# Which engine multiplies tokens by expert weights beside a recurrence, and the ranks of a planned schedule

## The chip, the cores and the metric

The kernel runs on one core of one Trainium2 chip, in one launch. The metric is device time in microseconds (us): the median of several executions. Besides, one execution is recorded by the hardware profiler, instruction by instruction; its own time and its span are given below. The engines are named as in the profile: PE is TensorE's matmul, PEld its weight load, DVE is VectorE, ACT is ScalarE, POOL is GpSimd, SP is SyncE.

## The reference

The input `x` is 8 sequences of 256 tokens of width 128, all in float32. Four stages follow each other, each added to its input after a layer normalisation:

```python
x = x + state_space(layernorm(x))      # a selective recurrence, 256 channels x 16 states
x = x + experts(layernorm(x))          # "p"
x = x + attention(layernorm(x))        # squared-relu attention with a gate, "a"
x = x + experts(layernorm(x))          # "r", with the same weights
```

The recurrence runs over the tokens of each sequence: `new = exp(A * d_t) * state + d_t * B_t * h_t`, and `y = sum_n new * C_t`. The expert layer has 8 experts of inner width 352; each token takes two of them, but all are computed and weighted:

```python
for e in range(8):
    w_e = sum(weights * (top_idx == e))            # 0 for experts not taken
    inter = (x @ w_up[e]) * silu(x @ w_gate[e])
    out = out + w_e[:, None] * (inter @ w_down[e])
```

## The kernel before, in words

The 8 sequences form four groups of two, so a group has 512 tokens. Activations are kept transposed: 128 features on the partitions, 512 tokens along the free dimension. For group g the work is cut into lanes (generators of operations):

- `s` (prelude, L516 on): normalisation, projection, convolution and step sizes of the recurrence. Its convolution on DVE, for groups 0 and 3, is L563.
- `m` (recurrence): 16 steps, each a multiplication (L744), a scan along tokens (L749) and a multiplication (L753) on DVE, all of 128 x 1024. The sum over states is made by DMAs that accumulate into a first buffer (lane `adder`, L716, issued on POOL's queue). Five buffers `st` exist; two hold the sums. ACT makes the decay factors (lane `feeder`, L697).
- `g`, `f`, `t`: the gate, the end of the recurrence (`y` on PE for groups 0 and 1, then a multiplication by the gate) and the projection back (`pb_m`).
- `r` (rest): expert layer p, attention a, expert layer r, with their normalisations and routers. Pieces of it are forked into lanes of their own. Group g's `r` starts after its `t` and after `r` of group g - 2.

So p0 means expert layer p of group 0. An expert layer folds the weight of an expert into the tokens: a row of weights, one per token, is broadcast to all partitions by a DMA (`fetched`, L969) into a buffer `wb` of 128 x 512, and `wb` is multiplied in place by the transposed tokens `xT` (`weighted`, L977). The up projection then reads `wb` in place of `xT`. The 8 x 352 inner columns are cut into 22 tiles of 128, so a tile can belong to two experts (then L993 instead of L986). For each tile PE makes the gate product (L487), ACT its silu (L960), PE the up product, DVE the product of both (`it`, L1000, one operand in PSUM), and PE the down product (L1006), two tiles later. The multiplication for an expert is issued when the expert two before it is through. Expert 0 of the layers named in `SOON` is not made in `weighted` but in the router's part, from PSUM (L940).

The order of all instructions is written by a planner (`Board`) at build time. It knows an estimated duration for each operation, keeps a time at which each engine becomes free, and each lane offers one operation. The one that can start first is taken; among those on the same engine that can start within the lane's `patience` of the first, the one with the lowest rank wins:

```python
first, lane = min(at, key=lambda x: x[0])
near = [
    l for t, l in at if l.op.engine == lane.op.engine and t <= first + l.patience
]
return min(near, key=lambda l: l.rank)
```

`RANKS` gives each kind of lane a rank per group (the group number breaks ties), and under "w" the patience of lanes `f` and of forked lanes. Where the planner sees PE idle for over 0.3 us ahead of a product, it fills the time with matmuls of the identity (L325). Each engine runs its instructions in the order written, and waits for semaphores where data come from elsewhere.

Of the kernel before, what the change touches and what calls it, by code (L numbers as in the profile page):

```python
# [10 lines left out]
ALU = mybir.AluOpType  # L11
# [84 lines left out]
def kernel(  # L96
# [27 lines left out]
    nc = tc.nc  # L124
# [23 lines left out]
    BEHIND = 2  # L148

    RANKS = {  # L150
        "s": [0, 4, 4, 1.5], "m": [1.5, 2, 3, 3.5],
        "g": [4, 0, 3.5, 2], "t": [0, 3.5, 3.5, 0.5],
        "r": [2, 0.5, 2.5, 0.5], "f": [2.5, 1.5, 4, 0.5], "w": [0, 0, 0.3, 0], "feeder": 5, "adder": 0,
    }
    SOON = ("p0", "p1", "r0", "p3", "r3")
    SPLIT = ()
    ENDS = 2
    assert E * F % P == 0 and all(cut >= P or cut % CG == 0 for _, cut in OWNER)
# [36 lines left out]
    for name, src in (  # L195
# [10 lines left out]
        n = src.shape[0]  # L206
# [75 lines left out]
    def ring(pool, shape, tag, name, bufs=1):  # L282

        held = rings.setdefault((pool.name, tag), [])
        free = held[-bufs].used if len(held) >= bufs else 0.0
        h = Held(pool.tile(shape, FP, tag=tag, name=name, bufs=bufs), free)
        held.append(h)
        return h
# [40 lines left out]
    def dve(us, out, ins, issue):  # L329
        return Op("DVE", us, out, ins, issue, lag=0.06)  # L330
# [4 lines left out]
    def pool(us, out, ins, issue):  # L335
        return Op("POOL", us, out, ins, issue, lag=0.06)

    def load(us, out, ins, issue, queue="SP", take=0.1):
        return Op(queue, take, out, ins, issue, lag=us)

    def mm(n):
        return 0.005 + 0.00167 * n
# [4 lines left out]
    def dve_us(n):  # L347
        return 0.08 + 0.0012 * n
# [22 lines left out]
    for k in range(K):  # L371
# [6 lines left out]
    PARTS = [  # L378
        [(b, b + 1) for b in range(n)] if g in SPLIT else [(0, n)] for g, n in enumerate(SIZES)
    ]  # L380
# [137 lines left out]
    def prelude(g):  # L518
# [64 lines left out]
        shut(ps)  # L583
        bc = Held(dram.tile([2 * N, G], FP, tag="bc", name=f"bc_{g}"))
        yield load(2.4, [bc], [ww], lambda: nc.sync.dma_start(bc.ap, xpj[R:XW, :]))


# [78 lines left out]
    def feeder():  # L666

        for g in range(NG):
# [6 lines left out]
            for q in range(N // NC):  # L675
# [4 lines left out]
                for tag, r0 in (("bt", q * NC), ("ct", N + q * NC)):  # L680
                    t = ring(scan, [P, NC, G], tag, f"{tag}_{g}_{q}", bufs=2)
                    yield load(4.0, [t], [bc], lambda: nc.sync.dma_start(
                        t.ap, bc.ap[r0 : r0 + NC, :].partition_broadcast(P)
                    ))
                    rows_at.append(t)
# [23 lines left out]
    def adder():  # L709

        while len(done & {f"f{g}" for g in range(NG)}) < NG:
            if not sums:
                yield None
                continue
            g, us, acc, st, into, of = sums.pop(0)
            yield load(us, [acc], [st], lambda: nc.gpsimd.dma_start(  # L716
                into, of, accum_op=ALU.add
            ), "POOL", 0.9)
            st.used = max(st.used, acc.ready)
            landed[g] = landed.get(g, 0) + 1  # L720
            if st is not acc:
                st.open = False
# [98 lines left out]
    def parted(g, tile):  # L821
        return tile, [Held(tile.ap[:, tokens(g, p)], tile.used) for p in range(len(PARTS[g]))]

    def whole(tile, parts):

        tile.ready = max(h.ready for h in parts)
        tile.used = max(h.used for h in parts)
        return tile
# [15 lines left out]
    def led_in(g, which, key, p, shared):  # L844
# [31 lines left out]
        if "we" not in shared:  # L876
# [8 lines left out]
            ]  # L885
            if f"{which}{g}" in SOON:
                shared["wb"] = parted(g, ring(
# [38 lines left out]

        if f"{which}{g}" not in SOON:
            return
# [16 lines left out]
    def moe(g, which, key, shared, ends):  # L945

        nm = f"{which}{g}"
        NT = SIZES[g] * TT
        G = NT * P
        xT, we = (whole(*shared[k]) for k in ("xT", "we"))  # L950
# [5 lines left out]
        def gate(i):  # L956
            gp = bank([P, G], f"gp_{nm}_{i}")
            yield pe(mm(G), [gp], [xT], product(gp.ap, [(wg_sb[:, i * P : (i + 1) * P], xT.ap)]))
            sg = ring(ffn, [P, G], f"sg{key}", f"sg_{nm}_{i}", bufs=SG)
            yield act(act_us(G), [sg], [gp], lambda: nc.scalar.activation(  # L960
                sg.ap, gp.ap, AF.Silu, bias=zero
            ), SILU)
            shut(gp)
            sgs[i] = sg
# [9 lines left out]
        def weighted(e):  # L974

            wb = wx[e]
            yield dve(dve_us(G), [wb], [xT], lambda: nc.vector.tensor_mul(wb.ap, wb.ap, xT.ap))  # L977

        def up(i, cols_of, sg, wa, wn, it, width):
# [49 lines left out]
        for i in range(LEAD):  # L1029
            yield from gate(i)  # L1030
        ahead = which + str(g) in SOON
        if not ahead:
# [3 lines left out]
        if not ahead:  # L1036
            yield from weighted(0)
        yield from weighted(1)

        dns = [  # L1040
# [4 lines left out]
        for i in range(NK - ENDS):  # L1045
            if i + LEAD < NK:
                yield from gate(i + LEAD)
            e, cut = OWNER[i]
            its[i] = tile_of(i)
            yield from up(i, everything, sgs.pop(i), wx[e], wx.get(e + 1), its[i], G)  # L1050
            if cut <= P:

                if e + WB < E:
                    yield from fetched(e + WB)
                if e + 2 < E:
                    yield from weighted(e + 2)
            if i >= BEHIND:
                it = its.pop(i - BEHIND)
                for p, dn in enumerate(dns):
                    yield from down(i - BEHIND, dn, it, tokens(g, p))  # L1060
# [250 lines left out]
```

## Time and profile before

| | us |
|---|---|
| median of 3 runs (759.11 to 759.85) | 759.33 |
| the profiled execution | 758.34 |
| its span, first to last instruction | 756.6 |
| PE busy, of which L325 | 737.7, 133.2 |
| DVE busy | 568.6 |
| ACT busy | 431.1 |
| POOL busy | 89.8 |

The clock granted to PE was 0.999 over the span. Busy times are unions over the span and say nothing of what waits for what; the filler L325 counts as busy PE. In the trace the 64 scans of the recurrences start between 41 and 511 us: those of group 0 from 41 to 118, of group 1 from 123 to 221, of group 2 from 235 to 373, of group 3 from 379 on. The first expert product of p0 is at 158 us, and the layers end as follows (L479, the addition of a layer's output): p0 at 232 us, p1 at 352, r0 at 419, r1 at 492, p2 at 542, p3 at 634, r2 at 704, r3 at 752.

### The profile page before, as it was taken

To read this page: it belongs to the slowest core of one execution; us is meant where nothing else is said; L and a number is where in the kernel's file an instruction comes from. 1 tells how busy PE (TensorE), PEld (TensorE's weight loads), DVE (VectorE), ACT (ScalarE), POOL (GpSimd) and SP (SyncE) were. 2 spreads that over 40 slices of the span, in tenths; PEclk is the share of its full clock that TensorE was granted. 3 is DMA by queue.
4 is the path that set the end of the run, shared out by engine and by line. 5 is a ranking of instruction groups with operands and counts; after the bars stand their busy time and mean duration, and the time that the engine had idled before them with its cause. 6 is when DMAs were issued, how large, how long until landed. Compare 5 with 4: busy or idle time off the path is not lost.

```text
span 756.6 us, 8464 instructions
## 1 busy us (share of the span) xinstructions
PE 737.7 (98%) x3093; PEld 403.6 (53%) x3093; DVE 568.6 (75%) x824; ACT 431.1 (57%) x570; POOL 89.8 (12%) x110
## 2 busy tenths in 40 slices
PE   4999999999999999999999999999999999999997
PEld 3877996853446744434754533443555434644343
DVE  2599999999999999899999998995735334354332
ACT  5578333799947879977876677742252322432220
POOL 2021110311112210002120110011100001000000
PEclk9999999999999999999999999999999999999999
DMA  8719795399763345655774666745011200000110
GB/s 260 209 57 220 169 219 162 98 228 218 166 171 84 76 124 133 166 133 138 176 170 96 159 161 179 160 102 109 2 42 27 72 15 14 15 29 29 47 36 14
DMA packets 38903, 88.63 MB, mean 117 GB/s; under 512 B 4339, under 2 KB 14542, under 8 KB 38862
## 3 DMA queue, kind: packets, MB, share of 16 engines
q0 software_dynamic: 9312, 30.94, 22.8%
q1 hardware_dynamic: 20624, 41.54, 17.2%
q10 hardware_dynamic: 8926, 15.61, 6.8%
q8 instruction: 24, 0.39, 0.2%
q14 instruction: 17, 0.14, 0.0%
HBM read 55.71 MB, written 1.44 MB: 76 GB/s over the span
## 4 chain that ended last, share of the span: by engine, by line
PE 78%; DVE 15%; ACT 3%; issue 2%; ACTq 0%; DVEq 0%
PE gp_r L487 10%; PE dn_r L1006 10%; PE dn_p L1006 9%; PE gp_p L487 9%; PE up_r L986 7%; PE up_p L986 7%; DVE st L749 6%; PE up_r L993 3%; DVE st L744 3%; PE up_p L993 3%; DVE st L753 2%; PE av_a L1197 2%; PE tp_p L325 1%; PE xpj L325 1%; PE v_a L1131 1%
## 5 line engine op out<-in xcount | busy, mean ns | idle before, releaser
L749 DVE TENSOR_TENSOR_SCAN st<-decay,st 128x1024 f32<-128x1024 f32 x64 | 147.8, 2309 | 2.5
L960 ACT ACTIVATE sg_r<-gp_r,zero 128x512 f32<-128x512 f32 x88 | 59.9, 687 | 109.8 <-PE gp_r L487 88.7
L57 ACT ACT_TABLE_LOAD x89 | 114.2, 1283 | 8.0 <-PE dn_r L1006 3.6
L697 ACT ACTIVATE decay<-dl,zero,a_sb 128x510 f32<-128x510 f32 x128 | 96.2, 804 | 36.9 <-DVE st L749 35.7
L1000 DVE TENSOR_TENSOR it_r<-up_r,sg_r 128x512 f32<-128x512 f32 x88 | 60.4, 687 | 66.7 <-PE up_r L986 42.3
L960 ACT ACTIVATE sg_p<-gp_p,zero 128x512 f32<-128x512 f32 x88 | 59.3, 685 | 62.5 <-PE gp_p L487 46.6
L1000 DVE TENSOR_TENSOR it_p<-up_p,sg_p 128x512 f32<-128x512 f32 x88 | 60.3, 686 | 43.4 <-PE up_p L986 29.4
L1006 PE MATMUL dn_p<-it_p,wd_sb 128*128 128x512 f32 x176 | 91.2, 605 | 0.6 <-DVE it_p L1000 0.6
L1006 PE MATMUL dn_r<-it_r,wd_sb 128*128 128x512 f32 x176 | 90.5, 603 | 0.0
L716 POOL DMA_DIRECT2D st<-st x58 | 50.4, 874 | 334.2 <-DVE st L753 303.7
L487 PE MATMUL gp_r<-xT_r,wg_sb 128*128 128x512 f32 x176 | 90.0, 597 | 0.0
L487 PE MATMUL gp_p<-xT_p,wg_sb 128*128 128x512 f32 x176 | 89.0, 594 | 0.0
L744 DVE TENSOR_TENSOR st<-bt,du 128x1024 f32<-128x1024 f32 x64 | 78.8, 1231 | 0.0
L753 DVE TENSOR_TENSOR st<-st,ct 128x1024 f32<-128x1024 f32 x64 | 78.1, 1221 | 0.7
L986 PE MATMUL up_p<-wb_p,wu_sb 128*128 128x512 f32 x128 | 65.1, 594 | 0.0
L986 PE MATMUL up_r<-wb_r,wu_sb 128*128 128x512 f32 x128 | 64.9, 592 | 0.0
L1006 PEld LDWEIGHTS dn_p<-it_p,wd_sb 128*128 128x128 f32 x176 | 31.3, 189 | 47.1 <-issue 36.3
L487 PEld LDWEIGHTS gp_r<-xT_r,wg_sb 128*128 128x128 f32 x176 | 32.6, 190 | 42.7 <-issue 37.4
L1006 PEld LDWEIGHTS dn_r<-it_r,wd_sb 128*128 128x128 f32 x176 | 31.6, 190 | 44.3 <-issue 39.5
L487 PEld LDWEIGHTS gp_p<-xT_p,wg_sb 128*128 128x128 f32 x176 | 32.8, 190 | 41.2 <-issue 36.3
L325 PEld LDWEIGHTS y<-ident 128*128 128x128 f32 x428 | 48.0, 192 | 1.2 <-PE dt L487 0.8
L325 PE MATMUL y<-ident 128*128 128x128 f32 x428 | 48.2, 275 | 0.0
(217 smaller groups left out, 853.1 us busy)
## 6 DMA issues: line engine op xcount, KB each, us to landing
st<-st POOLq DMA_DIRECT2D x54, 512.0 KB, 6.4
bt<-bc SPq DMA_DIRECT2D x32, 512.0 KB, 6.0
ct<-bc SPq DMA_DIRECT2D x32, 512.0 KB, 4.5
wb_r<-wrow_r ACTq DMA_DIRECT2D x30, 256.0 KB, 3.8
wb_p<-wrow_p ACTq DMA_DIRECT2D x29, 256.0 KB, 3.9
st<-h POOLq DMA_DIRECT2D x6, 256.0 KB, 4.9
wg_sb<-in_L_ffn_w_gate_dram SPq DMA_DIRECT2D x2, 704.0 KB, 4.7
wu_sb<-in_L_ffn_w_up_dram SPq DMA_DIRECT2D x2, 704.0 KB
```

The source lines that it names most:

```text
L57: self.load_tables(op.table)
L325: nc.tensor.matmul(ps[:, 0:n], lhsT=ident[:, 0:m], rhs=ident[:, 0:n], start=True, stop=True)
L487: nc.tensor.matmul(ps, lhsT=lhsT, rhs=rhs, start=(i == 0), stop=(i == len(terms) - 1))
L697: nc.scalar.activation(shaped[:, n, :, 1:], delta[c].ap.rearrange("p (b t) -> p b t", b=GB)[:, :, 1:], AF.Exp, bias=zero, scale=a_sb[:, c, ...
L716: yield load(us, [acc], [st], lambda: nc.gpsimd.dma_start(into, of, accum_op=ALU.add), "POOL", 0.9)
L744: yield dve(1.22, [st], [bt, du[c]], lambda: nc.vector.tensor_mul(st.ap, bt.ap, du[c].ap.unsqueeze(1).to_broadcast([P, NC, G])))
L749: yield dve(2.29, [st], [das[c]], lambda: nc.vector.tensor_tensor_scan(flat, das[c].ap.rearrange("p n t -> p (n t)"), flat, 0.0, ALU.mult, ...
L753: yield dve(1.22, [st], [ct], lambda: nc.vector.tensor_mul(st.ap, st.ap, ct.ap))
L960: yield act(act_us(G), [sg], [gp], lambda: nc.scalar.activation(sg.ap, gp.ap, AF.Silu, bias=zero), SILU)
L986: nc.tensor.matmul(ps.ap, lhsT=wu_sb[:, i * P : (i + 1) * P], rhs=wa.ap[:, cols_of], start=True, stop=True,)
L1000: yield dve(dve_us(width), [it], [ps, sg], lambda: nc.vector.tensor_mul(it.ap, ps.ap, sg.ap[:, cols_of]))
L1006: yield pe(mm(dn.ap.shape[1]), [dn], [it], lambda: nc.tensor.matmul(dn.ap, lhsT=wd_sb[:, i, :], rhs=it.ap[:, cols_of], start=(i == 0), sto ...
```

## The change

In the five expert layers p0, r0, p1, r1 and p2, the multiplication of `wb` by `xT` is issued on GpSimd (`nc.gpsimd.tensor_tensor`) instead of VectorE, and the planner is told a duration of 0.1 + 0.0024 x 512 = 1.33 us for it (0.69 us for the one on DVE). In p3, r2 and r3 it stays on DVE. The ranks change: of `s` for groups 1 and 3, `m` 2, `g` 2, `t` 2, `r` 0 and 1, `f` 1 and 2, the patience of group 1 (0 to 0.6) and the rank of the adder. A key "late" is added. The arithmetic is the same.

```diff
     RANKS = {
-        "s": [0, 4, 4, 1.5], "m": [1.5, 2, 3, 3.5],
-        "g": [4, 0, 3.5, 2], "t": [0, 3.5, 3.5, 0.5],
-        "r": [2, 0.5, 2.5, 0.5], "f": [2.5, 1.5, 4, 0.5], "w": [0, 0, 0.3, 0], "feeder": 5, "adder": 0,
+        "s": [0, 1.5, 4, 3], "m": [1.5, 2, 3.5, 3.5],
+        "g": [4, 0, 1.5, 2], "t": [0, 3.5, 4, 0.5],
+        "r": [1, 0, 2.5, 0.5], "f": [2.5, 3, 3, 0.5], "w": [0, 0.6, 0.3, 0], "late": 2, "feeder": 5, "adder": 1.5,
     }
     SOON = ("p0", "p1", "r0", "p3", "r3")
+
+    SPARED = ("p0", "r0", "p1", "r1", "p2")
...
+    def pool_us(n):
+        return 0.1 + 0.0024 * n
...
         def weighted(e):
 
             wb = wx[e]
+            if nm in SPARED:
+                yield pool(pool_us(G), [wb], [xT], lambda: nc.gpsimd.tensor_tensor(
+                    wb.ap, wb.ap, xT.ap, ALU.mult
+                ))
+                return
             yield dve(dve_us(G), [wb], [xT], lambda: nc.vector.tensor_mul(wb.ap, wb.ap, xT.ap))
```

## The prediction

> **What bounds the kernel now.** I read the page's busy times first, then the table of stages, then the chain, then single instructions on GpSimd (POOL) and VectorE (DVE).
>
> ```profile
> PE 737.7 (98%) x3093; PEld 403.6 (53%) x3093; DVE 568.6 (75%) x824; ACT 431.1 (57%) x570; POOL 89.8 (12%) x110
> PE 78%; DVE 15%; ACT 3%; issue 2%; ACTq 0%; DVEq 0%
> ```
>
> The first line has busy us, share and count of each engine; the second shares out the chain that ended last. TensorE (PE) seems full, but line 325 is the filler: multiplications of the identity that the planner puts wherever it sees PE idle. So the stages must be read with that line beside them. The first table has the busy time of every engine in five stretches, the second the filler alone.
>
> ```profile
> 40.00:128.00 88.00, 86.86 (x631) 73.77 (x630) 86.02 (x61) 47.02 (x64) 14.40 (x15) 1.00 0.69 169
> 128.00:160.00 32.00, 31.42 (x189) 23.27 (x189) 31.31 (x53) 22.29 (x31) 8.11 (x8) 1.00 0.57 131
> 160.00:280.00 120.00, 119.08 (x488) 64.02 (x487) 115.48 (x170) 96.41 (x124) 22.05 (x21) 1.00 0.62 153
> 280.00:520.00 240.00, 239.74 (x812) 110.25 (x813) 219.06 (x277) 173.64 (x213) 31.34 (x35) 1.00 0.62 147
> 520.00:756.00 236.00, 231.47 (x791) 108.66 (x789) 100.06 (x221) 68.94 (x106) 8.48 (x8) 1.00 0.11 30
> ```
> ```profile
> 160.00:280.00 120.00, 18.11 (x146) 17.71 (x144) 1.00 0.62 153
> 280.00:520.00 240.00, 10.96 (x90) 10.75 (x90) 1.00 0.62 147
> 520.00:756.00 236.00, 4.38 (x32) 4.20 (x32) 1.00 0.11 30
> ```
>
> After stretch and length the columns are PE, weight loads, DVE, ACT, POOL. From 40 to 160 us DVE is full (117.3 of 120) with the first recurrence and the start of the second, and there is no expert layer yet. From 160 to 280, beside recurrences, DVE is busy 115.5 of 120 and PE spends 18.1 us on filler: DVE sets the pace. From 280 to 520 DVE has 20.9 us idle and PE only 11.0 us of filler; both are near their limit. After 520 the recurrences are over and PE alone decides. So DVE time is worth its full price from 160 to 280, part of it to 520, nothing later, and no more than 18.1 + 11.0 = 29.1 us of filler can be won beside recurrences.
>
> **Part 1: the multiplication leaves DVE.** Line 977 has 59 instances. The layers named are p0, r0, p1 (seven each, expert 0 being made earlier, on DVE, at line 940) and r1, p2 (eight each): 37. They are the first 37 in the trace, 8 between 160 and 280 us and 29 to 526. One takes 682 ns (median), but back to back the next DVE instruction starts 0.60 us after it, so DVE is relieved of 37 x 0.60 = 22.2 us.
>
> **What comes back.** GpSimd has run no such multiplication, but it runs an addition of the same shape with two operands in SBUF, line 494: 1.27 us at least, 3.32 at most. Five of its eight lie beside a recurrence. Here are three of them (two GpSimd and DVE pairs, then a DVE multiplication of line 977 itself):
>
> ```profile
> 143.77 1.26 POOL L494 TENSOR_TENSOR x<-x,b_first 128x512 f32<-128x512 f32 x1 [0.71 <-ACT xn_m L437]
> 144.13 1.99 DVE L744 TENSOR_TENSOR st<-bt,du 128x1024 f32<-128x1024 f32 x1
> 253.38 1.26 POOL L494 TENSOR_TENSOR x<-x,b_first 128x512 f32<-128x512 f32 x1 [2.35 <-ACT xn_m L437]
> 253.53 1.41 DVE L899 TENSOR_TENSOR pair_p<-pr_p 128x256 f32<-128x256 f32 x1
> 358.03 1.39 POOL L494 TENSOR_TENSOR x<-x,b_back 128x512 f32<-128x512 f32 x1
> 358.45 1.53 DVE L977 TENSOR_TENSOR wb_r<-wb_r,xT_r 128x512 f32<-128x512 f32 x1
> ```
>
> Columns are start, duration, engine, line. Line 744 usually takes 1.22 us and took 1.99; line 899 takes 0.42 and took 1.41; line 977 takes 0.68 and took 1.53. The two others stretched a scan (2.29 us) to 3.18 and 2.76. Each of the five lengthened one DVE instruction, by 0.77, 0.99, 0.85, 0.89 and 0.47 us: mean 0.79. Lines 744 and 749 have no other long instance. The DVE operations hit read two operands in SBUF; at 639.57 us the same addition ran beside a line 1000 product, which reads one operand in PSUM, and that kept its 0.69 us. Most DVE time beside the moved work is of the first kind: lines 744, 749 and 753 alone fill 68 of the 115 busy us between 160 and 280.
>
> So a moved multiplication frees 0.60 us of DVE and takes about 0.79 back: +0.19 each, +7.0 us of DVE in all. The bounds are 0 taken back (it always falls beside line 1000), a gain of 22.2, and 1.27 taken back, a loss of 37 x 0.67 = 24.8; I take 0.79, since all five seen in this company paid. On the path: the eight before 280 us count fully, 8 x 0.19 = +1.5. The 29 later ones make 5.5, and 20.9 us of idle DVE time can cover them; I let a quarter through, +1.4 (5.5 without that cover).
>
> The Trainium skill, page "SBUF — State Buffer", section "SBUF: two separate sides", says that the shared ports are an exclusive lock held for the whole instruction, and that the other engine fully blocks. By that wording a loss could reach the whole 1.27 us each time; the rows show 0.47 to 0.99, because DVE often starts its instruction after GpSimd did, so the measured mean stands in the sum.
>
> **Latency of the product.** DVE gave it 0.68 us after the row's landing, GpSimd gives it 1.3 to 3.3. It is issued an expert ahead: 2.75 tiles of three products at 0.86 us (two matmuls 0.43 apart), 7.1 us of PE work. That hides it; uncovered, each would cost up to 2.6 us. I cost it at nothing. In r1 and p2 expert 0 goes this way too, with less lead, but another layer's matmuls are there to run.
>
> **GpSimd's queue.** It is in order. It gains 37 x 1.3 = 48 us and was 12% busy. Behind a multiplication waits the next accumulate (line 716, 0.86 us to issue, 6.4 to land), hence a buffer `st`. Three of the five rotate; a step comes every 360/42 = 8.6 us between 160 and 520 (42 scans of line 749), so a buffer has 25.7 us, of which 4.7 are work and 7.3 the accumulate. 13 us of slack hide up to 3.3 us of delay. Uncovered it would stall DVE by that delay. The other way round the multiplication stands behind accumulates that wait for DVE; this is the second rival.
>
> **Part 2: the ranks.** They reorder DVE, ACT and PE where several lanes are ready at the same instant; `late` is read nowhere. Three moves touch something the trace shows late.
> - `r` of group 0 goes from 2 to 1, below `s` of group 3 (1.5 to 3). At 262 to 269 us the six line 563 operations of prelude 3 (4.5 us) run on DVE ahead of r0's layernorm, while PE fills 26 times (3.06 us) ahead of `tp_r`. With r0 first that filler can go: 0 to -3.1, I take -1.5.
> - `f` of group 1 goes from 1.5 to 3, behind r0. Its `y` products (1.95 us of PE, twice) and with them tail 1 and layer p1 wait for PE's work in r0: 0 to +3.9, I take +1.0, since p0 is nearly over then.
> - Patience 0.6 for group 1's forks: PE may be left idle up to 0.6 us for about 29 of their steps, counted in the code: 0 to +17. Most find their operand there already; I take +1.0.
> - The rest (`s` 1 and 2, `m` 2, `g` 2, `t` 2, `f` 2, the adder) changes ties between lanes that are rarely ready together, or work for which the next stage waits on something else: 0 in the sum. An order that shifts everywhere can still move several us either way, and this is the largest unknown: -8 to +10, judged by the 9.1 us of PE filler between 360 and 440 us, where r0, a1 and r1 run short of products, and its mirror image.
>
> **Sum.** 758.34 (profiled execution: span 756.6 and 1.7 around it) + 1.5 + 1.4 - 1.5 + 1.0 + 1.0 = 761.7. The median of the runs, 759.33, is 1.0 above the profiled execution: **762.7 us**.
>
> **Rivals.**
> - *Faster.* The relief holds: GpSimd mostly runs beside line 1000, or the new order uses what DVE gets. For it: 18.1 us of filler between 160 and 280 with DVE full. Against it: five of five stretched. If a third of the 29.1 us of filler becomes products: 759.3 - 9.7 = 749.6. It decides from the point at which DVE loses under 0.5 us per multiplication, or at which the ranks alone win over 5 us. Chance 0.42.
> - *GpSimd's order.* Its accumulates wait for DVE 37 times between 160 and 520 us, 248.7 us in all and 12.5 at the longest. DVE will lag the written order by 29 us of blocking that the planner doesn't count, so a multiplication can stand behind an accumulate until its 7.1 us of cover is gone, and PE, in order too, stops: up to 12.5 - 7.1 = 5.4 us. Three such stops: 762.7 + 16 = 779. Chance 0.10.
> - *No change.* Blocking and relief cancel and the order wins as much as it loses: 759. Chance 0.09. That the edit does nothing is excluded: the layers' names match and the ranks are read.
>
> **How the numbers follow.** The forecast has 0.39, so slower by over 0.2% (1.5 us, about what a measurement of this kernel can tell from no change) has 0.39 + 0.10 = 0.49, within it 0.09, faster 0.42. The range reaches from the faster rival less half its gain again, 745, to just below the queue's stops, 776; the forecast's own range is 761 to 771.
>
> **What would show it.** Right: line 977's 37 instances on POOL at 1.3 us or more; lines 744, 749 and 753 with instances 0.5 to 1.2 us too long, 25 to 35 us in sum, about 10 of them before 280 us; DVE busy about 7 us more than 568.6; PE's filler between 160 and 520 near 29 us. Wrong: line 744 at 1.22 throughout, DVE busy down by 20 us, or filler there under 20 us. If POOL's accumulates wait as now but PE waits on `wb`, the queue is the cause.

## The result, and the profile after

The changed kernel takes 763.68 us (median of 4, 762.95 to 765.5) against 759.49 before in the same comparison: ratio 1.0059, 95% interval 1.004 to 1.0078. The prediction was 762.7. The profiled execution took 763.30 with a span of 761.5. The helper functions moved the lines: the filler is now L327, the steps of a recurrence L749 (multiplication), L754 (scan) and L758 (multiplication), the product `it` L1010, the down product L1016, the accumulate L721, and the moved multiplication is L983 on GpSimd (L987 where it stayed on VectorE).

First the page of the changed kernel: busy us, share and count of each engine, and the engines' shares of the chain that ended last ("issue" is time in which the engine waited for nothing that the profile shows).

```profile
PE 735.5 (97%) x3037; PEld 395.9 (52%) x3037; DVE 576.1 (76%) x787; ACT 431.7 (57%) x570; POOL 144.1 (19%) x147
PE 62%; DVE 22%; issue 9%; ACT 2%; POOL 2%; DMA 1%; DVEq 0%; ACTq 0%; POOLq 0%
```

Thirty-seven instructions have left DVE, and it is busy 7.5 us longer (568.6 before). Its share of the chain went from 15% to 22%, PE's from 78% to 62%, and "issue" from 2% to 9%. Next the stages (after start, end and length: PE, weight loads, DVE, ACT, POOL), and then the filler alone.

```profile
160.00:280.00 120.00, 114.68 (x466) 61.82 (x465) 115.64 (x144) 96.11 (x120) 35.91 (x30) 1.00 0.62 154
280.00:520.00 240.00, 236.17 (x782) 105.08 (x782) 226.31 (x265) 173.12 (x214) 70.04 (x64) 1.00 0.62 148
520.00:761.50 241.50, 237.44 (x792) 108.58 (x790) 101.55 (x222) 71.75 (x110) 10.14 (x9) 1.00 0.09 29
```
```profile
160.00:280.00 120.00, 18.29 (x149) 18.34 (x150) 1.00 0.62 154
280.00:520.00 240.00, 7.32 (x59) 6.92 (x58) 1.00 0.62 148
520.00:761.50 241.50, 0.83 (x6) 0.83 (x6) 1.00 0.09 29
```

From 160 to 280 us DVE is as full as before with 26 fewer instructions, and PE now stands still for 5.3 us (0.9 before), on top of as much filler. Between 280 and 520 the filler is 3.6 us less, but PE stands still for 3.8 us (0.3 before). Filler is idle time that the planner saw coming; standing still is what it did not expect. The groups of instructions by line and form (count, then busy us and mean ns) say where DVE's time went:

```profile
L754 DVE TENSOR_TENSOR_SCAN st<-decay,st 128x1024 f32<-128x1024 f32 x64 | 156.0, 2437 | 3.3 <-DVE st L749 0.5
L749 DVE TENSOR_TENSOR st<-bt,du 128x1024 f32<-128x1024 f32 x64 | 90.8, 1419 | 0.0
L983 POOL TENSOR_TENSOR wb_p<-wb_p,xT_p 128x512 f32<-128x512 f32 x22 | 35.6, 1635 | 7.6 <-DMA wb_p<-wrow_p 7.6
L983 POOL TENSOR_TENSOR wb_r<-wb_r,xT_r 128x512 f32<-128x512 f32 x15 | 22.6, 1509 | 12.6 <-DMA wb_r<-wrow_r 12.6
```

The same 64 scans took 147.8 us before, the same 64 multiplications 78.8. Single instructions of the changed kernel show how (start, duration, engine, line):

```profile
178.53 1.56 POOL L983 TENSOR_TENSOR wb_p<-wb_p,xT_p 128x512 f32<-128x512 f32 x1
178.15 3.04 DVE L749 TENSOR_TENSOR st<-bt,du 128x1024 f32<-128x1024 f32 x1
197.14 2.78 POOL L983 TENSOR_TENSOR wb_p<-wb_p,xT_p 128x512 f32<-128x512 f32 x2
196.76 3.73 DVE L637 TENSOR_TENSOR dl<-dl,ww 128x512 f32<-128x512 f32 x1
```

A multiplication of 1.22 us took 3.04 beside one of GpSimd's, and one of 0.69 took 3.73 beside two in a row. Below, *stretch* is the sum over DVE instructions of what each took above the median of its line and shape, where that is over 0.1 us. It was 4.0 us before (all beside GpSimd's additions) and is 34.2 now: 30.2 more, 0.82 for each of the 37. Not all of the instructions hit read two tensors: six are the normalisation L427, with one tensor and scalars per partition as input, at 0.65 to 1.39 us instead of 0.34, 4.0 us in sum. None is a product `it` (L1010, one operand in PSUM): 19 of these ran beside a multiplication on GpSimd for over 0.2 us, and the longest took 0.69.

PE feels it through the product `it`. The first line is the wait of the weight load ahead of a down product in the kernel before, the second in the changed one (total us, times, longest):

```profile
PEld dn_p L1006 <- DVE it_p L1000: 8.4, 14, 1.4
```
```profile
PEld dn_p L1016 <- DVE it_p L1010: 16.4, 20, 2.3
```

### The profile page after: what moved, and what is told of

Read it like the earlier page. It is cut to its first block, busy times and chain, and to the rows that moved or that the text cites. A ratio compares the mean times of both kernels' runs of the same rounds, so it can differ in the third digit from the quotient of the medians.

```text
span 761.5 us, 8378 instructions
## 1 busy us (share of the span) xinstructions
PE 735.5 (97%) x3037; PEld 395.9 (52%) x3037; DVE 576.1 (76%) x787; ACT 431.7 (57%) x570; POOL 144.1 (19%) x147
## 3 DMA queue, kind: packets, MB, share of 16 engines
q0 software_dynamic: 9312, 30.94, 22.6%
## 4 chain that ended last, share of the span: by engine, by line
PE 62%; DVE 22%; issue 9%; ACT 2%; POOL 2%; DMA 1%; DVEq 0%; ACTq 0%; POOLq 0%
PE dn_p L1016 8%; PE gp_r L492 8%; DVE st L754 8%; PE dn_r L1016 8%; PE gp_p L492 8%; PE up_p L996 6%; PE up_r L996 6%; DVE st L749 5%; DVE st L758 4%; PE up_p L1003 3%; PE up_r L1003 2%; PE av_a L1207 1%; DVE it_r L1010 1%; PE xpj L327 1%; DMA st<-st 1%
## 5 line engine op out<-in xcount | busy, mean ns | idle before, releaser
L754 DVE TENSOR_TENSOR_SCAN st<-decay,st 128x1024 f32<-128x1024 f32 x64 | 156.0, 2437 | 3.3 <-DVE st L749 0.5
L1010 DVE TENSOR_TENSOR it_r<-up_r,sg_r 128x512 f32<-128x512 f32 x88 | 59.6, 684 | 67.8 <-PE up_r L996 49.8
L721 POOL DMA_DIRECT2D st<-st x58 | 50.9, 882 | 272.6 <-DVE st L758 205.5
L1010 DVE TENSOR_TENSOR it_p<-up_p,sg_p 128x512 f32<-128x512 f32 x88 | 59.7, 683 | 49.3 <-PE up_p L996 27.1
L1016 PE MATMUL dn_p<-it_p,wd_sb 128*128 128x512 f32 x176 | 91.0, 606 | 4.0 <-DVE it_p L1010 4.0
L1016 PE MATMUL dn_r<-it_r,wd_sb 128*128 128x512 f32 x176 | 90.3, 601 | 1.2 <-DVE it_r L1010 1.2
L749 DVE TENSOR_TENSOR st<-bt,du 128x1024 f32<-128x1024 f32 x64 | 90.8, 1419 | 0.0
L758 DVE TENSOR_TENSOR st<-st,ct 128x1024 f32<-128x1024 f32 x64 | 80.5, 1258 | 0.9
L1016 PEld LDWEIGHTS dn_p<-it_p,wd_sb 128*128 128x128 f32 x176 | 31.2, 189 | 51.1 <-issue 30.7
L1016 PEld LDWEIGHTS dn_r<-it_r,wd_sb 128*128 128x128 f32 x176 | 31.7, 190 | 42.4 <-issue 35.1
L327 PEld LDWEIGHTS y<-ident 128*128 128x128 f32 x470 | 52.8, 192 | 1.2 <-PE dt L492 0.8
L327 PE MATMUL y<-ident 128*128 128x128 f32 x470 | 53.1, 275 | 0.0
```

The source lines that it names most:

```text
L327: nc.tensor.matmul(ps[:, 0:n], lhsT=ident[:, 0:m], rhs=ident[:, 0:n], start=True, stop=True)
L721: yield load(us, [acc], [st], lambda: nc.gpsimd.dma_start(into, of, accum_op=ALU.add), "POOL", 0.9)
L749: yield dve(1.22, [st], [bt, du[c]], lambda: nc.vector.tensor_mul(st.ap, bt.ap, du[c].ap.unsqueeze(1).to_broadcast([P, NC, G])))
L754: yield dve(2.29, [st], [das[c]], lambda: nc.vector.tensor_tensor_scan(flat, das[c].ap.rearrange("p n t -> p (n t)"), flat, 0.0, ALU.mult, ...
L758: yield dve(1.22, [st], [ct], lambda: nc.vector.tensor_mul(st.ap, st.ap, ct.ap))
L1010: yield dve(dve_us(width), [it], [ps, sg], lambda: nc.vector.tensor_mul(it.ap, ps.ap, sg.ap[:, cols_of]))
```

## The experiments

The theory: GpSimd's multiplications hold up DVE for as long as they relieve it or longer, DVE paces PE here, and the ranks matter little. The main rival: blocking is absorbed and the ranks make the loss. A second one: GpSimd's queue in order makes `wb` late. Ratios are to the kernel before in the same comparison, whose median lay between 759.1 and 759.7 us; all kernels but the two named memset compute the same.

| kernel | us | ratio to before (95%) | DVE busy | stretch |
|---|---|---|---|---|
| before | 759.5 | 1 | 568.6 | 4.0 |
| changed | 763.68 | 1.0059 (1.004 to 1.0078) | 576.1 | 34.2 |
| engine_only | 786.3 | 1.0351 (1.0336 to 1.0365) | 575.0 | 32.3 |
| ranks_only | 765.74 | 1.0081 (1.0068 to 1.0094) | 569.8 | 3.9 |
| memset | 750.76 | 0.9888 (0.9873 to 0.9903) | 548.1 | 3.7 |
| memset2 | 750.92 | 0.9889 (0.9876 to 0.9903) | 548.3 | 4.2 |
| same_order_dve | 754.84 | 0.9935 (0.9923 to 0.9948) | 568.0 | 3.9 |
| gp_p0 | 759.56 | 0.9997 (0.9989 to 1.0006) | 573.2 | 13.4 |
| gp_rest | 757.65 | 0.9978 (0.9969 to 0.9988) | 570.5 | 24.5 |
| old_ranks_dve | 778.13 | 1.0243 (1.023 to 1.0257) | 568.4 | 4.2 |
| undo_w1 | 784.31 | 1.0329 (1.0314 to 1.0345) | 580.6 | 38.5 |
| undo_r0_s3 | 778.54 | 1.0256 (1.024 to 1.0271) | 584.3 | 42.1 |
| blocking_told | 774.74 | 1.0203 (1.0186 to 1.022) | 585.9 | 42.4 |
| searched_dve | 750.03 | 0.9875 (0.9858 to 0.9891) | 567.8 | 4.8 |

### Each half of the change alone

```diff
# engine_only: the changed kernel with the ranks of before
# ranks_only: the changed kernel with no layer spared
-    SPARED = ("p0", "r0", "p1", "r1", "p2")
+    SPARED = ()
```

> The old ranks, and the 37 multiplications on GpSimd. If the shared ports give back what VectorE is relieved of (the prediction's theory): VectorE instructions stretched by 25 to 35 us in sum, VectorE busy 574 to 577 us, and 760 to 764 us, 0 to 4 us slower than before. If the ranks alone made the kernel slower and the blocking is absorbed (rival one): 755 to 759 us, at or below before.

> The new ranks, and all multiplications on VectorE. Prediction's theory: the ranks are worth about +0.5 us in sum, so 758 to 762 us, and no VectorE instruction longer than usual beyond the 4 us in sum of before. Rival one (the ranks are the whole loss): 763 to 766 us.

Neither theory had this. The multiplications on GpSimd with the old ranks cost 27 us, the new ranks without them 6.6, and both together 4.2. The stretch with the old ranks is 32.3 us and DVE busy 575.0, as expected; the time is 22 us above the expected 760 to 764. So the halves don't add up: the planner writes the order from the ranks and from the price and engine that it is told, and that order had to be parted from the engine that does the work.

### The order without the engine

```diff
# same_order_dve (the changed kernel's plan); old_ranks_dve (the same with the ranks of before)
-                yield pool(pool_us(G), [wb], [xT], lambda: nc.gpsimd.tensor_tensor(
+                yield pool(pool_us(G), [wb], [xT], lambda: nc.vector.tensor_tensor(
```

The planner still believes in GpSimd and 1.33 us; the instruction goes to VectorE at that place.

> The changed kernel's order as the planner wrote it with GpSimd's 1.33 us, but the 37 multiplications issued on VectorE at that place. Prediction's theory: VectorE gets 22 us of work back and loses 30 us of blocking, so 758 to 763 us, a little faster than the changed kernel, although its order was planned for another engine. If the relief of VectorE is real and blocking harmless: slower than the changed kernel, 767 us or more.

> The old ranks, the planner told that the 37 multiplications run on GpSimd for 1.33 us, but all issued on VectorE. It parts the 786.3 us of old ranks with GpSimd: if the order is what is bad, 774 to 781 us (786.3 less the 9 us that the engine costs in the other order); if blocking weighs more in that order, 757 to 768.

The changed kernel's order with all work on VectorE takes 754.84 us, 4.3 us less than before (759.09 in that comparison) and 8.8 us less than the changed kernel (9.4 by the two ratios, as the runs of before differ a little). That is below the expected 758 to 763: the theory had the direction, not the size. The order with old ranks and the new price takes 778.13: there the order is what is bad, as the first reading had it, and GpSimd adds 786.3 - 778.1 = 8.2 us. So in both orders the engine costs 8 to 9.4 us, and with VectorE doing all of it the four orders stand so:

| | planned on VectorE | planned on GpSimd |
|---|---|---|
| old ranks | 759.5 | 778.1 |
| new ranks | 765.7 | 754.8 |

The old ranks are good with the engine and price of VectorE, the new ones with GpSimd's, and each set loses 11 to 19 us with the other. PE's filler shows it; first old_ranks_dve, then same_order_dve:

```profile
160.00:280.00 120.00, 26.37 (x218) 26.05 (x218) 1.00 0.67 162
280.00:520.00 240.00, 15.45 (x130) 15.27 (x130) 1.00 0.60 142
520.00:640.00 120.00, 5.65 (x50) 5.38 (x50) 1.00 0.08 23
```
```profile
160.00:280.00 120.00, 19.50 (x158) 19.35 (x158) 1.00 0.64 155
280.00:520.00 240.00, 6.11 (x48) 5.91 (x48) 1.00 0.62 148
520.00:640.00 120.00, 0.00 (x0) 0.00 (x0) 1.00 0.10 29
```

The sums are 47.5 and 25.6 us: 21.9 of the 22.9 us between the spans (776.2 and 753.3) are idle time that the planner itself had written in.

### Is it the reading, the occupancy or the lateness?

```diff
# memset; memset2 writes 0.2 and then 0.1. What is left out is the product itself.
-                yield pool(pool_us(G), [wb], [xT], lambda: nc.gpsimd.tensor_tensor(
-                    wb.ap, wb.ap, xT.ap, ALU.mult
-                ))
+                yield pool(pool_us(G), [wb], [xT], lambda: nc.gpsimd.memset(wb.ap, 0.1))
```

> The changed kernel in its own order, but GpSimd writes a constant into wb in place of multiplying it, so it reads no SBUF there (the experts' outputs are then those of a constant input). Prediction's theory: with no second reader the stretching of VectorE falls from 34 us to under 8, VectorE busy from 576 to about 548 us, and the time by 4 to 10 us, to 754 to 760. Rival one: stretching is absorbed elsewhere, and the time stays at 762 to 765. Rival two (GpSimd's queue in order is what delays): the write is shorter than the product, about 0.5 us by the other writes of this kernel, so the time falls by 2 us or less with PE still waiting on wb.

> The changed kernel's order; GpSimd writes two constants into wb, one after the other, in place of the product (the experts' input is a constant). GpSimd is then held about as long as by a product (two writes of 0.5 to 0.9 us against 1.57), but reads nothing. If the shared read path is the cost: VectorE stretched by under 8 us, 750 to 754 us, within 3 us of the single write. If GpSimd's occupancy or the lateness of wb were the cost: 757 to 763 us.

Groups of the single write (memset), then of the double one (memset2):

```profile
L754 DVE TENSOR_TENSOR_SCAN st<-decay,st 128x1024 f32<-128x1024 f32 x64 | 147.2, 2301 | 3.3 <-DVE st L749 0.5
L749 DVE TENSOR_TENSOR st<-bt,du 128x1024 f32<-128x1024 f32 x64 | 78.6, 1228 | 0.0
L983 POOL MEMSET wb_p<- 128x512 f32 x22 | 15.5, 707 | 19.0 <-DMA wb_p<-wrow_p 19.0
```
```profile
L749 DVE TENSOR_TENSOR st<-bt,du 128x1024 f32<-128x1024 f32 x64 | 78.7, 1230 | 0.0
L983 POOL MEMSET wb_p<- 128x512 f32 x44 | 27.0, 615 | 17.0 <-DMA wb_p<-wrow_p 14.5 <-PE dn_p L1014 1.3
L983 POOL MEMSET wb_r<- 128x512 f32 x30 | 19.0, 634 | 14.2 <-DMA wb_r<-wrow_r 12.6 <-PE tp_r L457 0.7
```

In an unchanged order the stretch is gone and the time falls by 13 us, more than the 4 to 10 expected. Two writes in place of one, 46 us on GpSimd against 58 for the products, change nothing (750.92 against 750.76). So GpSimd's occupancy is not the cost. Nor is the lateness of `wb`: PE's waits for it sum to 2.2 us in the changed kernel and to 2.3 in the same order on VectorE, and the second rival falls. What costs is an operation on GpSimd that reads SBUF beside DVE; the writes leave out the reading and the arithmetic together, and no run parts these two. The Trainium skill, page "SBUF — State Buffer", section "Who interferes with whom", states that a DVE instruction with two SBUF inputs contends with a GpSimd instruction that reads SBUF and not with one that only writes it; the 34.2 us of stretch against 3.7 and 4.2 agree.

### Early and late multiplications

```diff
# gp_p0: the seven of p0 on GpSimd, 30 on VectorE. gp_rest: the other way round ("!=")
-                yield pool(pool_us(G), [wb], [xT], lambda: nc.gpsimd.tensor_tensor(
+                yield pool(pool_us(G), [wb], [xT], lambda: (nc.gpsimd if nm == "p0" else nc.vector).tensor_tensor(
```

> The changed kernel's order, the seven multiplications of p0 on GpSimd, the other 30 on VectorE. The prediction let the early ones, from 160 to 280 us, count in full: at 30 us of stretching for 37 (0.82 each, less 0.60 of relief) that is +1.5 us over the 754.8 of all on VectorE, 755.5 to 758. If stretched instructions do not matter for the path here: 754 to 755.

> The same order, with p0's seven on VectorE and the other 30 on GpSimd. If, as the prediction had it, idle VectorE time covers three quarters of the later ones: +1.4 us over 754.8, 755 to 757. If nearly all of VectorE's net loss reaches the end also beyond 280 us: +5 to +8 us, 760 to 763.

The order is that of same_order_dve, so 754.84 is the base. The seven of p0 cost 4.7 us, the thirty others 2.8 (3.3 if the ratios are compared); together 7.5 of the 8.8. Both miss: the early ones cost more than expected, the late ones less than the rival reading and more than the prediction's. The stretch tells why. For the seven it is 13.4 - 3.9 = 9.5 us, 1.35 each, which less 0.60 of relief is 5.3 us; for the thirty 24.5 - 3.9 = 20.6, 0.69 each, which is 2.6 us. DVE busy rises by 5.2 and 2.5. So for p0 DVE's net loss reaches the end nearly one to one, and the early multiplications lose more of it. For the thirty others the medians say the same, less surely: the twelve executions spread from 755.82 to 759.78, the profiled one is the lowest of them, and the intervals of the two ratios leave 1.6 to 4.9 us.

PE's wait for a late `it` moves with the engine. The weight loads ahead of down products waited in the layers p as follows, first in same_order_dve, then in gp_p0:

```profile
PEld dn_p L1016 <- DVE it_p L1010: 5.4, 10, 0.8
```
```profile
PEld dn_p L1016 <- DVE it_p L1010: 16.1, 19, 2.3
```

With p0's seven on GpSimd the wait in the layers p is nearly that of the changed kernel (16.4), and the one in the layers r is 1.3 us, as in same_order_dve. With the thirty others there it is the other way round: 5.9 in the layers p, 6.3 in the layers r (6.2 in the changed kernel).

### The ranks one by one, and a planner that is told

```diff
# undo_w1 (the rest of RANKS, here and below, is left out: ...)
-        ... "w": [0, 0.6, 0.3, 0] ...
+        ... "w": [0, 0, 0.3, 0] ...
# undo_r0_s3
-        "s": [0, 1.5, 4, 3], ... "r": [1, 0, 2.5, 0.5] ...
+        "s": [0, 1.5, 4, 1.5], ... "r": [2, 0, 2.5, 0.5] ...
# blocking_told
+                yield dve(0.82, [], [], lambda: None)
                 yield pool(pool_us(G), [wb], [xT], lambda: nc.gpsimd.tensor_tensor(
```

> The changed kernel with the patience of group 1's forked lanes back at 0. The prediction charged the patience with +1.0 us, so without it 762 to 763 us. Rival: the patience is a large part of what makes the new order good (the written order gains 4.3 us over before when VectorE does the work): 768 us or more without it.

> The changed kernel with the ranks of group 0's expert lanes and of prelude 3 as before (2 and 1.5), so prelude 3 goes first again. The prediction credited the move with 1.5 us: 764 to 766 us without it. Rival: ranks are worth whatever the whole order comes to, not the local filler: outside 760 to 768.

> The changed kernel, its planner told of 0.82 us of VectorE time for each of GpSimd's multiplications (the measured mean of the stretching), in front of each. If the loss comes from blocking that the planner does not know: a planner that knows it writes an order that loses less, under 761 us. If the planner's price merely shuffles the order: anywhere from 760 to 780 us, with the same 30 us of stretching.

Taking back the patience costs 20.6 us over the changed kernel, taking back r0 and prelude 3 costs 14.9: in both the rival reading holds, by far. Both orders also have more stretch (38.5 and 42.1 us against 34.2) and more filler (137.8 and 133.5 us over the span against 126.1), so these figures mix what the order costs PE with what it makes GpSimd cost DVE. With `f` of group 1 alone put back to 1.5 the planner writes the same program. The planner that was told of the blocking wrote a worse order (774.74) with more stretch (42.4). That the ranks were not chosen for that price is one reading; whether ranks chosen for it would do better was not tried.

### A faster version

```diff
# searched_dve: same_order_dve with other ranks (the lines that these replace are left out)
+    RANKS = {'s': [0, 1.5, 4, 3], 'm': [2.0, 1.0, 3.5, 3.5], 'g': [4, 4.5, 1.5, 2], 't': [0, 3.5, 4, 0.5],
+             'r': [1, 0, 2.5, 0.5], 'f': [2.0, 3, 0.0, 0.5], 'w': [0, 0.6, 0, 0], 'feeder': 5, 'adder': 0.5}
+    SOON = ('p0', 'p1')
```

> An attempt at a faster version: order planned with GpSimd's price and issued on VectorE, as in the kernel of 754.8 us, with ranks searched further for that order (s as changed; m 2, 1, 3.5, 3.5; g 4, 4.5, 1.5, 2; f 2, 3, 0, 0.5; patience 0, 0.6, 0, 0; adder 0.5) and expert 0 made early for p0 and p1 alone. If that order holds with VectorE's real load: 750 to 754 us. If a tuned order is only good for the load it was planned with, as the other orders suggest: 755 to 765 us.

750.03 us, 1.25% faster than before and 1.8% faster than the changed kernel. The order holds with VectorE's real load, although it was planned for another engine.

## Why the prediction was right or wrong

**The number was right, partly by luck.** The sum had +2.9 us for the engine and +0.5 for the order. In the order that was written the engine costs 8.8 (763.68 - 754.84), and the order wins 4.3 (759.09 - 754.84): +4.6 by these two, +4.2 measured in the first comparison, +3.4 predicted. The engine's term was 5.9 us too small and the order's 4.8 too high, and these cancel. The mechanism behind the direction was right, but its predicted size was not enough for it: 2.9 us of loss against the 4.3 that the order won would have made the kernel faster.

**DVE's balance: right in its sums.** Relief of 0.60 each: DVE is busy 19.9 us less with the write-only version than in the same order on VectorE, 0.54 each. Blocking of 0.79 each: 0.82 measured. DVE busy +7 us: +7.5. Stretch of 25 to 35 us in the three lines of the recurrence, 0.5 to 1.2 each: 24.8 there, up to 1.83 each, and 9.4 in other lines, 34.2 in all; about 10 before 280 us from the moved multiplications: 10.0. That a product `it` pays nothing held. That only instructions with two operands in SBUF pay did not: L427 paid too.

**What of it reaches the end: the mis-sized term.** The eight early ones were put at 8 x 0.19 = 1.5 us; the seven of p0 alone measured 4.7. The exposure in full was right, but the mean of five additions does not hold there: 1.35 each. Of the later ones a quarter was let through, 1.4 of 5.5 us, with 20.9 us of idle DVE time as the cover. Their net loss was only 2.6 us, 0.09 each instead of 0.19, and 2.8 measured: within the noise of that run all of it came through. PE waits for the `it` that comes late, as the waits above show, and idle DVE time elsewhere in the stage did not help. The three kernels of one order show how unlike DVE time can be: from 548.1 to 568.0 us of it the time rises by 4.1 us, from 568.0 to 576.1 by 8.8. A reading that no run tests by itself: the first 20 us mostly fall into gaps of that order, the last 8 are instructions that end late.

**Latency and queue at nothing: right.** PE's waits for a late `wb` are 2.2 us in the changed kernel, no more than with VectorE in the same order, and the double write shows no price of occupancy.

**The ranks step by step: wrong.** `f` of group 1 was charged +1.0 and does nothing. The patience was charged +1.0 and taking it back costs 20.6 us in the changed kernel. r0 before prelude 3 was credited with 1.5, and taking it back costs 14.9; nor did r0 begin sooner, its layernorm being at 275 us against 267. The step that failed is that a rank was priced by the filler beside it. A rank changes which instruction is next, every later choice follows from that, and the effects do not add: the two moves taken back would sum to 35.5 us where all ranks together, also with GpSimd, are worth 22.6 (786.3 - 763.7). The allowance of -8 to +10 us for the whole order was the useful part, and -4.3 lies in it.

**The rivals.** *Faster* needed DVE to lose under 0.5 us per multiplication, or ranks worth over 5; it lost 0.82, and the order won 4.3, just short. Of the filler between 160 and 520 us 3.5 us went (25.6 against 29.1), but PE stands still there 8.0 us longer. *GpSimd's order* did not come about: PE's longest wait for `wb` is 1.3 us where the rival had stops of 5.4, and the accumulates wait for DVE less than before, 30 times and 157.4 us between 160 and 520 (37 and 248.7).

## What to carry to other kernels

Before an operation is moved from a full VectorE to GpSimd, look in the trace for any GpSimd operation that reads SBUF beside VectorE work: what it adds to its neighbours is the price, and here it was more than the relief. Look at the place that the moved work will have, too: the same multiplication cost 1.35 us of DVE time each in p0 and 0.69 in the other layers. When a change moves both an engine and a planned order, issue the work on the old engine in the new order: that one line parted a loss of 8.8 us from a gain of 4.3. Price a reordering by the whole order that comes out, not by the stall beside the edit, and do not count idle time of the same stage as cover for an instruction that ends late without looking at who waits for it.

## What the runs showed that was not expected

The stretch can be longer than GpSimd's multiplication by itself. The shortest products took 1.26 us. In the changed kernel 20 of the 37 start less than 0.9 us after an accumulate's issue on GpSimd began; these take 1.60 us in the mean and stretch DVE by 1.00, up to 1.83, while the other 17 stretch it by 0.62. In the pair at 178 us the VectorE instruction had even started first, and still took 1.82 us longer. Six of p0's seven in the run with p0 alone stand behind an accumulate in this way, which fits their 1.35 each. But the order of starting goes with it: all five multiplications L749 that lost 1.81 to 1.83 us had started 0.34 to 0.39 us before GpSimd's product, each behind an accumulate, while instructions that started after a product behind an accumulate lost 0.55 to 1.23. Whether the accumulate's issue or the order of starting is the cause was not tested by a run of its own.
